# A third tile picked by matmuls in one step of four of a graph attention layer

## The chip, the core and the metric

The kernel runs on one core of a Trainium2 chip, in one launch. The metric is the device time of that launch in microseconds (us); the lower the better. The core has five engines that work side by side, each through its own queue of instructions in order: PE (matmuls, with its weight loads shown as a row of their own, PEld), DVE (vector operations), ACT (activations and copies), POOL (here it issues the indirect gathers) and SP (here it issues the other DMAs). They wait for each other by semaphores only. SBUF is the working memory, PSUM the memory that matmuls write to.

## What is computed

A graph has 6250 nodes with 64 features each and 206250 edges (200000 drawn ones and a loop at each node), sorted by destination. For each edge the key and the value of its source, the query of its destination and a projection of its own features make four scores (heads); the messages are summed by destination, added to the node's features and normalised. Cut to what matters:

```python
Qh = (x @ Wq.T + bq).reshape(n, H, D)          # n = 6250, H = 4, D = 16
Kh = (x @ Wk.T + bk).reshape(n, H, D)
Vh = (x @ Wv.T + bv).reshape(n, H, D)
Ee = (edge_attr @ We.T + be).reshape(-1, H, D)
score = (Kh[src] * Qh[dst] * (1.0 / np.sqrt(D)) * Ee).sum(-1)
score = jnp.exp(jnp.clip(score, -5.0, 5.0))
msg = Vh[src] * score[..., None]
wV = jax.ops.segment_sum(msg, dst, num_segments=n)
x = _layernorm(x + wV.reshape(n, H * D), axis=-1)
```

## The kernel before

**Tiles, groups, steps.** The edges are cut into 1612 tiles of 128, one edge to a partition. Eight tiles are a group, two groups (16 tiles) a step; the last eight steps have one group each, so there are 105 steps. The kernel computes k and v of all nodes first and writes them to a table in memory (`kv_tab`).

**Sources by gather.** k and v of a tile's 128 sources come by one indirect DMA for each tile (`gather_kv`, L389 to L393), which POOL issues. They land in one of five step buffers (`kvs`, KVB = 5). In step s the gathers of step s + 4 are put into POOL's queue; the buffer that they go to was read last by the message of step s - 1.

**Sources by matmul.** In the steps s = 4 to 94 (`picks_in`) the last two tiles of step s + 2 get k and v in another way: their rows of x are *picked* by matmuls, and `gather` leaves these tiles out. x is held in SBUF as three bf16 parts that add up to fp32 (`parts`): row 50 p + b of x stands on partition p in block b, with 50 blocks. For a picked tile:

- `sources` (ACT, L449) computes the source number less 50 p for each edge and each p, and `sources_turned` (PE, L458) transposes that into PSUM (`from_b`), so that p is the partition;
- `hots` (DVE, L465) compares it with the 50 block numbers and so makes 50 one-hot matrices of 128 x 128, in two halves of 25, an instruction each;
- `picks` (PE, L475) multiplies each of them with a block of the parts, 50 matmuls that accumulate in `rows3`, also in two halves;
- `picked` (DVE) adds the three parts, `picked_turned` (PE, ACT) transposes the rows, and `picked_kv` (PE, ACT) multiplies them with the weights of k and v and copies the result to the step's buffer.

**The rest of a step.** `spread` (PE, L518) with `onehot_rows` (ACT) makes the one-hot matrices by which `queries` (PE, L558) fetches the queries; `edges` (PE, L377 and L380) computes the projected edge features; `products` and `scores` (DVE, L565 to L574) and an exponential (ACT, L575) make the scores; `message` (DVE, L582) the messages, which `minus` (PE L593, ACT L595) splits into three bf16 parts; `sums` (PE, L601) adds them by destination with the one-hots of `onehot_edges` (DVE, L548), and `add` (DVE, L615) puts them into accumulators. About every second step a block of 128 destinations is complete and is closed (`close`, `spreads`, from L631 on).

**The order.** It is written out by hand in the loop from L671 on, with no scheduler behind it: each engine runs its instructions in the order of the calls. The PSUM tile `edges` writes to has one buffer, so the next step's edges wait for this step's products. The order within a step, with the engine's own work named once each: spread and sums (PE), sources turned (PE), products (DVE), picked (DVE), edges (PE), first picks (PE), scores, add, message (DVE), the second half of the edges and the minus matmuls around the second picks (PE), two hots, the one-hots of the edges and the two hots of the next step (DVE), k and v of the picked rows, third picks, queries, fourth picks (PE), closing (DVE).

Of the kernel before, what the change touches and what calls it, by code (L numbers as in the profile page):

```python
# [7 lines left out]
F32 = mybir.dt.float32  # L8
BF16 = mybir.dt.bfloat16
I32 = mybir.dt.int32  # L10
AF = mybir.ActivationFunctionType
# [3 lines left out]
P = 128  # L15
N = 6250
C = 64
# [21 lines left out]
KVB = 5  # L39
XG = 4  # L40
TB = 8
M0 = 4
PAD = N
SPARE = N + 1
# [13 lines left out]
def groups_of(s):  # L58
    return range(STEPS[s][0], STEPS[s][0] + STEPS[s][1])
# [6 lines left out]

def picks_in(s):
    return M0 <= s <= LAST


def about_where(g):
# [20 lines left out]
def tile_gnn(ctx: ExitStack, tc: tile.TileContext, x, xT, wT, bias, beT, weT, eT, src, dst, dst_rows,  # L92
# [308 lines left out]
    with tc.If(rv == 0) as branch:  # L401

        with tc.tile_pool(name="work", bufs=2) as work, \
# [2 lines left out]
                tc.tile_pool(name="psum", bufs=1, space=bass.MemoryType.PSUM) as psum:  # L406
            TO, OH, PE, PQ, M3, PA = ({} for _ in range(6))
            small = fixed.tile([P, 4 * P], F32, name="small")
            col, from0, from1 = (small[:, i * C:(i + 1) * C].bitcast(BF16) for i in range(3))
            from_b = from0, from1  # L410
            score_all = small[:, 3 * C:3 * C + 2 * G * H]
            pa = small[:, 4 * C:7 * C].rearrange("p (i c) -> p i c", i=3)
            nc.tensor.transpose(col, row_b[:, 0:1].to_broadcast([P, P]), ident_b)

            parts = accp.tile([P, NB, 3, C], BF16, name="parts")
# [6 lines left out]
            for i in range(2):  # L422
                nc.vector.tensor_copy(src_f[:, :, i],
                                      src_i[:, t0 + i:t0 + i + 2 * G * (n_picks - 1) + 1:2 * G])
            pick = fixed.tile([P, 4 * P], F32, name="pick")
            rows3 = pick[:, :6 * C].rearrange("p (k i c) -> p k i c", k=2, i=3)
            HOT, FAR, X = {}, {}, {}
# [15 lines left out]
            def table_parts_rest(b, rest):  # L443
# [2 lines left out]
                nc.scalar.activation(parts[:NX, b:b + n, 1], rest, AF.Copy)  # L446
                nc.vector.tensor_sub(parts[:NX, b:b + n, 2], rest, parts[:NX, b:b + n, 1])

            def sources(s, i):  # L449

                if picks_in(s):
                    FAR[s, i] = work.tile([P, P], BF16, name="far")
                    nc.scalar.activation(FAR[s, i], row50, AF.Identity,
                                         bias=src_f[:, s - M0, i:i + 1], scale=-1.0)

            def sources_turned(s, i):  # L458
                if picks_in(s):
                    nc.tensor.transpose(from_b[i], FAR.pop((s, i)), ident_b)  # L460

            def blocks(h):
# [1 line left out]

            def hots(s, i, h):  # L465

                if picks_in(s):
                    HOT[s, i, h] = work.tile([P, NB // 2, P], BF16, name="hot", bufs=4)
                    shape = [P, NB // 2, P // 2, 2]
                    nc.vector.tensor_tensor(  # L470
                        HOT[s, i, h].rearrange("p b (a c) -> p b a c", c=2),
                        pairs(from_b[i])[:, None].to_broadcast(shape),
                        block2[:, blocks(h), None, :].to_broadcast(shape), op=OP.is_equal)

            def picks(s, i, h):  # L475
                if picks_in(s):
                    hot = HOT.pop((s, i, h))
                    for k in range(NB // 2):
                        b = h * NB // 2 + k
                        nc.tensor.matmul(rows3[:, i], hot[:, k, :], parts[:, b], start=b == 0,  # L480
                                         stop=b == NB - 1)

            def picked(s):

                if picks_in(s):
                    xp = work.tile([P, 2, C], F32, name="xp")
                    nc.vector.tensor_reduce(xp, rows3.rearrange("p k i c -> p k c i"), axis=AX.X,
                                            op=OP.add)
                    X[s] = xp

            def picked_turned(s):
                if picks_in(s):
                    room = psum.tile([P, G, P], F32, name="pb")
                    nc.tensor.transpose(room[:, 0, :], X[s].rearrange("p k c -> p (k c)"), ident)
                    xe = work.tile([P, P], F32, name="xe")
                    nc.scalar.activation(xe, room[:, 0, :], AF.Copy)
                    X[s] = xe, room[:, 4:6, :]

            def picked_kv(s):
                if picks_in(s):  # L500
                    xe, kv = X.pop(s)
                    nc.tensor.matmul(kv, ones_b, bkv_p[:, :2], start=True, stop=False,
                                     skip_group_check=True)
                    nc.tensor.matmul(kv, xe, wkv, start=False, stop=True, skip_group_check=True)  # L504
                    nc.scalar.activation(kvs[(s + 2) % KVB][:, 2 * G - 2:, :], kv, AF.Copy)

            def gather(s):
                for g in groups_of(s):
                    for j in range(tiles_of(g)):
                        if not picks_in(s - 2) or g == STEPS[s][0] or j < G - 2:  # L510
                            gather_kv(g, j)


# [74 lines left out]
            def minus(s, msg, i):  # L588

                n = tiles_in(s)  # L590
                for lo in range(0, n, G):
                    hi = min(n, lo + G)
                    nc.tensor.matmul(msg[:, lo:hi, :], minus_b, M3[s][:, lo:hi, i, :], start=False,  # L593
                                     stop=True, skip_group_check=True)
                nc.scalar.activation(M3[s][:, :n, i + 1, :], msg[:, :n, :], AF.Copy)  # L595
# [75 lines left out]
            for s in range(NS):  # L671
                more = s + 1 < NS
                for g in groups_of(s):
                    if g % LG == 0 and g + 2 * LG < NG:
                        fetch_edges(g // LG + 2)
                if s + 2 < NS:
                    for g in groups_of(s + 2):
                        fetch_queries(g)
                nexts = list(groups_of(s + 1)) if more else []
                if more:  # L680
                    onehot_rows(nexts[0], spread(nexts[0]))
                    onehot_rows_rest(nexts[0])
                if s:
                    sums(s - 1)
                sources_turned(s, 1)
                sources_turned(s + 1, 0)
                if nexts[1:]:
                    onehot_rows(nexts[1], spread(nexts[1]))
                making = [b for b in range(s * 2 * TB, (s + 1) * 2 * TB, TB) if b < NB]
                if making:  # L690
                    rest = table_parts(making[0])
                prod = products(s)
                picked(s - 1)
                if more:
                    edges(s + 1, 0)
                picks(s, 0, 0)
                score = scores(s, prod)
                if nexts[1:]:
                    onehot_rows_rest(nexts[1])
                if s:  # L700
                    add(s - 1)
                msg = message(s, score)
                if s + KVB - 1 < NS:
                    gather(s + KVB - 1)
                picked_turned(s - 1)
                if nexts[1:]:
                    edges(s + 1, 1)
                minus(s, msg, 0)
                hots(s, 1, 0)
                picks(s, 0, 1)  # L710
                minus(s, msg, 1)
                picked_kv(s - 1)
                if not more:

                    close(B - 2)
                    spreads(B - 2)
                hots(s, 1, 1)
                picks(s, 1, 0)
                sources(s + 1, 1)
                sources(s + 2, 0)  # L720
                if more:
                    if nexts[0] * G % KEYS == 0:
                        keys(nexts[0] * G)
                    onehot_edges(s + 1)
                    queries(s + 1)
                picks(s, 1, 1)
                hots(s + 1, 0, 0)
                hots(s + 1, 0, 1)
                if more:

                    while closed < B - 2 and due[closed] <= s:
                        close(closed)
                        spreads(closed)
                        closed += 1
                    if closed in BATCHES and closed > scaled:
                        roots(scaled, closed)
                        scales(scaled, closed)
                        scaled = closed
                    for _ in range(3):
                        if normed < scaled:  # L740
                            norm(normed)
                            normed += 1
                for i, b in enumerate(making):
                    if i:
                        rest = table_parts(b)
                    table_parts_rest(b, rest)
# [175 lines left out]
```

## Time and profile before

| | us |
|---|---|
| median of 3 runs | 1808.31 |
| lowest and highest of them | 1808.10, 1808.62 |
| the profiled execution's own time | 1808.39 |
| its span, from first to last instruction | 1806.6 |

| engine | busy us | share of the span | instructions |
|---|---|---|---|
| PE, matmuls | 1641.5 | 91% | 15751 |
| PE, weight loads | 1370.4 | 76% | 15751 |
| DVE | 1481.7 | 82% | 1695 |
| ACT | 912.0 | 50% | 1313 |
| POOL | 1351.8 | 75% | 1442 |

A group of the page is written as line, engine, operation, output and input by the program's names, count, busy time and mean duration, and then the idle time just before these instructions with what ended it. "issue" there is time in which the engine waited for nothing that the profile shows. Matmuls are pipelined: the duration of one record is longer than the distance to the next, so costs of PE are better read from start to start. A line of the timeline has start, duration and instruction, and in brackets the idle time before it.

### The profile page before, as it was taken

Reading aid. Unit: us, or ns where it says so; the run is one execution under the profiler, and the core shown is the slowest. Engines: PE = TensorE matmul, PEld = TensorE weight load, DVE = VectorE, ACT = ScalarE, POOL = GpSimd, SP = SyncE. Lnnn points to the kernel's source line nnn. Section 1 sums busy time; section 2 is a strip of 40 time slices with the busy share of each in tenths; the row PEclk is TensorE's granted clock in tenths of the full one; section 3 lists DMA queues with packets and bytes.
Section 4 is the critical chain, followed back from the end, with each engine's and each line's share of the span. In section 5 each row is a group of like instructions: output and inputs, shape, how many; then the busy total and the mean of one; then the engine's idle time right before and its main releaser. Section 6 shows DMA issues by size and latency. Waiting matters only on the chain.

```text
span 1806.6 us, 38129 instructions
## 1 busy us (share of the span) xinstructions
PE 1641.5 (91%) x15751; PEld 1370.4 (76%) x15751; DVE 1481.7 (82%) x1695; ACT 912.0 (50%) x1313; POOL 1351.8 (75%) x1442
## 2 busy tenths in 40 slices
PE   8979999999999998999899898989999999999864
PEld 8547888888877777777777787877777778777632
DVE  6459999999988898888888888888988888888554
ACT  4465555555545454544545444455444545445443
POOL 7777777777777777777777777777777777777774
PEclk9968999999999999999999999999999999999855
DMA  8343323333323333332333323323332332332331
GB/s 239 112 120 92 92 80 104 80 101 83 92 79 93 91 84 90 99 81 81 92 91 90 80 79 93 91 79 98 84 92 80 92 91 79 91 91 79 89 79 45
DMA packets 106532, 166.30 MB, mean 92 GB/s; under 512 B 67501, under 2 KB 67822, under 8 KB 106236
## 3 DMA queue, kind: packets, MB, share of 16 engines
q0 software_dynamic: 45760, 92.76, 19.6%
q1 hardware_dynamic: 60204, 70.01, 13.5%
q8 instruction: 125, 2.05, 0.5%
q10 hardware_dynamic: 384, 1.00, 0.3%
q14 instruction: 59, 0.48, 0.1%
HBM read 156.32 MB, written 7.33 MB: 91 GB/s over the span
## 4 chain that ended last, share of the span: by engine, by line
PE 31%; POOL 28%; DVE 19%; issue 14%; DMA 4%; ACT 3%; DVEq 0%; SPq 0%; POOLq 0%; ACTq 0%
POOL kv L391 28%; PE pick L480 15%; DVE hot L470 7%; PE pe L380 4%; DMA kv<-kv_tab,src_i 4%; PE pq L593 2%; DVE prod L565 2%; DVE prod L566 2%; PE small L601 2%; DVE pq L582 2%; DVE small L572 2%; PE pb L518 2%; DVE acc L615 1%; PE pb L504 1%; PE pe L377 1%
## 5 line engine op out<-in xcount | busy, mean ns | idle before, releaser
L391 POOL DMA_INDIRECT kv<-kv_tab,src_i x1398 | 1319.7, 944 | 426.1 <-issue 403.5
L480 PE MATMUL pick<-parts,hot 128*128 128x192 bf16 x9100 | 825.6, 249 | 0.0
L480 PEld LDWEIGHTS <-hot 128*128 128x128 bf16 x9100 | 769.6, 99 | 38.0
L470 DVE TENSOR_TENSOR hot<-small,block 128x3200 bf16<-128x3200 bf16 x364 | 645.9, 1816 | 0.8 <-PE pick L480 0.8
L535 ACT ACTIVATE to<-pb,minus_row 126x1024 bf16<-126x1024 f32 x202 | 222.8, 1103 | 372.7 <-PE pb L518 368.7
L380 PEld LDWEIGHTS pe<-we_sb,et 128*128 128x128 f32 x1612 | 213.2, 206 | 152.9 <-issue 136.8
L595 ACT ACTIVATE msg<-pq 128x1024 bf16<-128x1024 f32 (+2 forms) x210 | 207.8, 990 | 219.7 <-PE pq L593 219.7
L565 DVE TENSOR_TENSOR prod<-kv,pq 128x1024 f32<-128x1024 f32 (+2 forms) x105 | 123.6, 1177 | 191.7 <-DMA kv<-kv_tab,src_i 92.7
L380 PE MATMUL pe<-we_sb,et 128*128 128x128 f32 x1612 | 254.3, 305 | 0.0
L540 ACT ACTIVATE to<-to,one_p 126x1024 bf16<-126x1024 bf16 x202 | 230.6, 1142 | 3.5
L377 PE MATMUL pe<-be_p,ones_b 3*128 3x512 bf16 x202 | 80.0, 396 | 104.8 <-DVE prod L566 104.8
L601 PEld LDWEIGHTS <-of 128*128 128x128 bf16 x1612 | 145.1, 102 | 30.9 <-issue 7.8
L601 PE MATMUL small<-msg,of 128*128 128x192 bf16 x1612 | 161.5, 256 | 0.5 <-ACT msg L595 0.5
L593 PE MATMUL pq<-msg,minus_b 128*128 128x512 bf16 x404 | 128.1, 396 | 30.8 <-ACT msg L585 16.6
L585 ACT ACTIVATE msg<-pq 128x1024 bf16<-128x1024 f32 (+2 forms) x105 | 103.9, 990 | 96.9 <-DVE pq L582 96.9
L572 DVE TENSOR_REDUCE small<-prod 128x64 f32<-128x1024 f32 (+2 forms) x105 | 123.6, 1177 | 13.3 <-PE small L460 7.5
L518 PE MATMUL pb<-key_rows,ident_b 112*128 112x512 bf16 x403 | 127.7, 399 | 2.8 <-ACT to L535 2.8
L566 DVE TENSOR_TENSOR prod<-prod,pe 128x1024 f32<-128x1024 f32 (+2 forms) x105 | 123.6, 1177 | 3.6
L582 DVE TENSOR_TENSOR pq<-kv,small 128x1024 f32<-128x1024 f32 (+2 forms) x105 | 123.5, 1176 | 1.4 <-ACT small L575 1.4
L548 DVE TENSOR_TENSOR of<-small,key 128x2048 bf16<-128x2048 bf16 (+2 forms) x105 | 123.2, 1173 | 0.3
L575 ACT ACTIVATE small<-small 128x64 f32<-128x64 f32 (+2 forms) x105 | 21.7, 207 | 131.0 <-DVE small L574 130.5
L558 PEld LDWEIGHTS <-to 126*128 126x128 bf16 x1612 | 63.5, 101 | 25.1 <-issue 24.9
(128 smaller groups left out, 992.1 us busy)
## 6 DMA issues: line engine op xcount, KB each, us to landing
et<-in_eT SPq DMA_DIRECT2D x100, 512.0 KB
kv<-kv_tab,src_i POOLq DMA_INDIRECT x1398
qw<-q_tab SPq DMA_DIRECT2D x202, 15.8 KB
kv_tab<-kv_sb SPq DMA_DIRECT2D x5, 640.0 KB
q_tab<-q SPq DMA_DIRECT2D x5, 480.0 KB
acc<-in_x SPq DMA_DIRECT2D x48, 32.0 KB
out<-y SPq DMA_DIRECT2D x48, 32.0 KB
raw<-in_x SPq DMA_DIRECT2D x6, 250.0 KB
```

The lines of the kernel that those rows point to most:

```text
L380: nc.tensor.matmul(pe[:, 2 * u:2 * u + 2, :], et[:, u, :], we_sb, start=False, stop=u == n // 2 - 1, skip_group_check=True)
L391: nc.gpsimd.indirect_dma_start(out=kv_of(g)[:, j, :], out_offset=None, in_=kv_tab[:, :], in_offset=bass.IndirectOffsetOnAxis(ap=src_i[:, t ...
L470: nc.vector.tensor_tensor(HOT[s, i, h].rearrange("p b (a c) -> p b a c", c=2), pairs(from_b[i])[:, None].to_broadcast(shape), block2[:, bl ...
L480: nc.tensor.matmul(rows3[:, i], hot[:, k, :], parts[:, b], start=b == 0, stop=b == NB - 1)
L518: nc.tensor.matmul(pb[:, b:b + 4, :], ident_b[:NR2, g // 2:g // 2 + 1].to_broadcast([NR2, P]), key_rows[:, g % 2, b * P:(b + 4) * P], star ...
L535: nc.scalar.activation(TO[g][:, :n, :], pb[:3 * W, :n, :], AF.Square, bias=minus_row3[:3 * W])
L540: nc.scalar.activation(TO[g][:, :n, :], TO[g][:, :n, :], AF.Relu, bias=one_p[:3 * W], scale=-1.0)
L565: nc.vector.tensor_mul(prod[:, :n, :], kvs[s % KVB][:, :n, :C], PQ[s][:, :n, :])
L566: nc.vector.tensor_mul(prod[:, :n, :], prod[:, :n, :], PE[s][:, :n, :])
L593: nc.tensor.matmul(msg[:, lo:hi, :], minus_b, M3[s][:, lo:hi, i, :], start=False, stop=True, skip_group_check=True)
L595: nc.scalar.activation(M3[s][:, :n, i + 1, :], msg[:, :n, :], AF.Copy)
L601: nc.tensor.matmul(PA[s], OH[s][:, j, :], M3[s][:, j], start=j == 0, stop=j == n - 1)
```

## The change

In every fourth step of those that pick (steps 4, 8, ... 92, `picks_third`), a third tile is picked by matmuls, the one ahead of the pair in the buffer, and its gather is left out.

The third tile has an index of its own, 2, in `sources`, `sources_turned`, `hots` and `picks`. Its source numbers have a place of their own in the PSUM tile `small` (so `score_all` and `pa` move up by one place), and a table `src_f3`. Its picks run after the first tile's and before the second's and write to the second tile's region of `rows3`. Therefore the second tile's picks, which otherwise stand around the queries, come at the end of such a step, behind a new reduction `picked_third` on DVE, which reads the region before it is used again. The third tile's first hot stands at the end of the step before, behind the next step's two; its second hot stands between the two of the second tile. The reduced rows share one tile with those of the pair; they are transposed by a matmul of their own, and k and v of all three come from one bias matmul and two products and leave PSUM by one copy. The buffers for `hot` go from 4 to 6 and those for `far` from 2 to 3.

```diff
+def picks_third(s):
+    return picks_in(s) and s % THIRD == 0
+
+def is_picked(g, j):
+    s = g // 2
+    return picks_in(s - 2) and g == groups_of(s)[-1] and j >= (G - 3 if picks_third(s - 2) else G - 2)
...
-            col, from0, from1 = (small[:, i * C:(i + 1) * C].bitcast(BF16) for i in range(3))
-            from_b = from0, from1
-            score_all = small[:, 3 * C:3 * C + 2 * G * H]
-            pa = small[:, 4 * C:7 * C].rearrange("p (i c) -> p i c", i=3)
+            col, *from_b = (small[:, i * C:(i + 1) * C].bitcast(BF16) for i in range(4))
+            score_all = small[:, 4 * C:4 * C + 2 * G * H]
+            pa = small[:, 5 * C:8 * C].rearrange("p (i c) -> p i c", i=3)
...
+            def wanted(s, i):
+                return picks_third(s) if i == 2 else picks_in(s)
...
-                    FAR[s, i] = work.tile([P, P], BF16, name="far")
+                    FAR[s, i] = work.tile([P, P], BF16, name="far", bufs=3)
...
-                    HOT[s, i, h] = work.tile([P, NB // 2, P], BF16, name="hot", bufs=4)
+                    HOT[s, i, h] = work.tile([P, NB // 2, P], BF16, name="hot", bufs=6)
...
-                        nc.tensor.matmul(rows3[:, i], hot[:, k, :], parts[:, b], start=b == 0,
-                                         stop=b == NB - 1)
+                        nc.tensor.matmul(rows3[:, min(i, 1)], hot[:, k, :], parts[:, b],
+                                         start=b == 0, stop=b == NB - 1)
+
+            def picked_third(s):
+                if picks_third(s):
+                    X[s] = work.tile([P, 3, C], F32, name="xp")
+                    nc.vector.tensor_reduce(X[s][:, 0], rows3[:, 1].rearrange("p i c -> p c i"),
+                                            axis=AX.X, op=OP.add)
...
+                    if picks_third(s):
+                        nc.tensor.transpose(room[:C, 1, :], X[s][:, 0], ident)
+                    nc.scalar.activation(xe[:, 0], room[:, 0, :], AF.Copy)
+                    if picks_third(s):
+                        nc.scalar.activation(xe[:C, 1], room[:C, 1, :], AF.Copy)
...
+                    lo = 0 if picks_third(s) else 1
+                    nc.tensor.matmul(kv[:, lo:], ones_b, bkv_p[:, lo:3], start=True, stop=False,
+                                     skip_group_check=True)
+                    nc.tensor.matmul(kv[:, 1:], xe[:, 0], wkv, start=False, stop=lo == 1,
+                                     skip_group_check=True)
+                    if lo == 0:
+                        nc.tensor.matmul(kv[:, 0], xe[:C, 1], wkv[:C, 0], start=False, stop=True,
+                                         skip_group_check=True)
+                    nc.scalar.activation(kvs[(s + 2) % KVB][:, 2 * G - 3 + lo:, :], kv[:, lo:], AF.Copy)
...
-                        if not picks_in(s - 2) or g == STEPS[s][0] or j < G - 2:
+                        if not is_picked(g, j):
                             gather_kv(g, j)
...
                 sources_turned(s + 1, 0)
+                sources_turned(s + 1, 2)
...
                 hots(s, 1, 0)
+                hots(s, 2, 1)
                 picks(s, 0, 1)
+                picks(s, 2, 0)
                 minus(s, msg, 1)
+                picks(s, 2, 1)
                 picked_kv(s - 1)
...
                 hots(s, 1, 1)
-                picks(s, 1, 0)
+                if not picks_third(s):
+                    picks(s, 1, 0)
                 sources(s + 1, 1)
                 sources(s + 2, 0)
+                sources(s + 2, 2)
...
-                picks(s, 1, 1)
+                if not picks_third(s):
+                    picks(s, 1, 1)
                 hots(s + 1, 0, 0)
+                picked_third(s)
+                if picks_third(s):
+                    picks(s, 1, 0)
+                    picks(s, 1, 1)
                 hots(s + 1, 0, 1)
+                hots(s + 1, 2, 0)
```

More of the change, by code (lines that the diff above doesn't have):

```diff
@@ L41 @@
 TB = 8
+THIRD = 4
 M0 = 4
@@ L424, in tile_gnn @@
                                       src_i[:, t0 + i:t0 + i + 2 * G * (n_picks - 1) + 1:2 * G])
+            src_f3 = accp.tile([P, (LAST - M0) // THIRD + 1], F32, name="src_f3")
+            assert M0 % THIRD == 0
+            nc.vector.tensor_copy(src_f3, src_i[:, t0 - 1:t0 + 2 * G * (LAST - M0):2 * G * THIRD])
             pick = fixed.tile([P, 4 * P], F32, name="pick")
@@ L447, in table_parts_rest @@
                 nc.vector.tensor_sub(parts[:NX, b:b + n, 2], rest, parts[:NX, b:b + n, 1])
+            def wanted(s, i):
+                return picks_third(s) if i == 2 else picks_in(s)
             def sources(s, i):
-                if picks_in(s):
-                    FAR[s, i] = work.tile([P, P], BF16, name="far")
-                    nc.scalar.activation(FAR[s, i], row50, AF.Identity,
-                                         bias=src_f[:, s - M0, i:i + 1], scale=-1.0)
+                if wanted(s, i):
+                    FAR[s, i] = work.tile([P, P], BF16, name="far", bufs=3)
+                    at = src_f3[:, (s - M0) // THIRD:][:, :1] if i == 2 else src_f[:, s - M0, i:i + 1]
+                    nc.scalar.activation(FAR[s, i], row50, AF.Identity, bias=at, scale=-1.0)
             def sources_turned(s, i):
-                if picks_in(s):
+                if wanted(s, i):
                     nc.tensor.transpose(from_b[i], FAR.pop((s, i)), ident_b)
@@ L465, in hots @@
             def hots(s, i, h):
-                if picks_in(s):
-                    HOT[s, i, h] = work.tile([P, NB // 2, P], BF16, name="hot", bufs=4)
+                if wanted(s, i):
+                    HOT[s, i, h] = work.tile([P, NB // 2, P], BF16, name="hot", bufs=6)
                     shape = [P, NB // 2, P // 2, 2]
@@ L475, in picks @@
             def picks(s, i, h):
-                if picks_in(s):
+                if wanted(s, i):
                     hot = HOT.pop((s, i, h))
@@ L479, in picks @@
                         b = h * NB // 2 + k
-                        nc.tensor.matmul(rows3[:, i], hot[:, k, :], parts[:, b], start=b == 0,
-                                         stop=b == NB - 1)
+                        nc.tensor.matmul(rows3[:, min(i, 1)], hot[:, k, :], parts[:, b],
[5 more added lines that the diff above has]
+                                            axis=AX.X, op=OP.add)
             def picked(s):
                 if picks_in(s):
[L486 to L489, printed above, removed]
+                    if s not in X:
+                        X[s] = work.tile([P, 3, C], F32, name="xp")
+                    nc.vector.tensor_reduce(X[s][:, 1:], rows3.rearrange("p k i c -> p k c i"),
+                                            axis=AX.X, op=OP.add)
             def picked_turned(s):
@@ L493, in picked_turned @@
                     room = psum.tile([P, G, P], F32, name="pb")
[L494 to L497, printed above, removed]
+                    xe = work.tile([P, 2, P], F32, name="xe")
+                    nc.tensor.transpose(room[:, 0, :], X[s][:, 1:].rearrange("p k c -> p (k c)"), ident)
+                    if picks_third(s):
[3 more added lines that the diff above has]
+                        nc.scalar.activation(xe[:C, 1], room[:C, 1, :], AF.Copy)
+                    X[s] = xe, room[:, 4:7, :]
             def picked_kv(s):
@@ L501, in picked_kv @@
                     xe, kv = X.pop(s)
-                    nc.tensor.matmul(kv, ones_b, bkv_p[:, :2], start=True, stop=False,
+                    lo = 0 if picks_third(s) else 1
+                    nc.tensor.matmul(kv[:, lo:], ones_b, bkv_p[:, lo:3], start=True, stop=False,
                                      skip_group_check=True)
-                    nc.tensor.matmul(kv, xe, wkv, start=False, stop=True, skip_group_check=True)
-                    nc.scalar.activation(kvs[(s + 2) % KVB][:, 2 * G - 2:, :], kv, AF.Copy)
+                    nc.tensor.matmul(kv[:, 1:], xe[:, 0], wkv, start=False, stop=lo == 1,
[4 more added lines that the diff above has]
+                    nc.scalar.activation(kvs[(s + 2) % KVB][:, 2 * G - 3 + lo:, :], kv[:, lo:], AF.Copy)
             def gather(s):
```

## The prediction

> **What bounds the kernel now.** I read the page's groups first, then the starts of the first product of each step (DVE, L565) along the timeline, then busy time by stretch, then single steps. The groups of the page:
>
> ```profile
> L391 POOL DMA_INDIRECT kv<-kv_tab,src_i x1398 | 1319.7, 944 | 426.1 <-issue 403.5
> L480 PE MATMUL pick<-parts,hot 128*128 128x192 bf16 x9100 | 825.6, 249 | 0.0
> L470 DVE TENSOR_TENSOR hot<-small,block 128x3200 bf16<-128x3200 bf16 x364 | 645.9, 1816 | 0.8 <-PE pick L480 0.8
> ```
>
> POOL waits for no consumer: its idle time is 0.3 us of issue after each gather. Its first gather starts at 43.1 and its last at 1787.7, so the pitch is 1744.6 / 1397 = 1.249 us. That chain, and 18.0 us behind it, is the span. A step with two picked tiles has 14 gathers: 17.48 us.
>
> But the kernel did not always run at that pace. The first product starts at 145.47 in step 4, 176.34 in step 6, 333.31 in step 16, 474.53 in step 25 and 1680.72 in step 94. From step 6 to 25 that is 15.69 us a step; from 25 to 94 it is 17.48. Early on the steps work off the gathers fetched ahead; from step 25 they wait for new ones. Two stretches, one of each kind:
>
> ```profile
> core 0: us, PE busy (x) PEld busy (x) DVE busy (x) ACT busy (x) POOL busy (x), PEclk, DMA share, GB/s
> ...
> 165.00:300.00 135.00, 135.00 (x1416) 115.60 (x1414) 127.59 (x130) 73.73 (x104) 102.07 (x109) 1.00 0.33 88
> ...
> 900.00:1050.00 150.00, 138.34 (x1422) 117.66 (x1422) 126.84 (x128) 73.16 (x103) 113.42 (x121) 0.99 0.31 84
> ```
>
> In the first, PE has no idle time and DVE 5.5%. So there are two limits: POOL's 17.48 us, and a computing pace of 15.69 us a step that shows only early. The second decides the change. The timeline of steps 8 and 9 shows what sets it:
>
> ```profile
> 207.73 1.22 DVE L565 TENSOR_TENSOR prod<-kv,pq 128x1024 f32<-128x1024 f32 x1 [0.29 <-DMA kv<-kv_tab,src_i]
> ...
> 210.35 0.39 PE L377 MATMUL pe<-be_p,ones_b 3*128 3x512 bf16 x1
> ...
> 222.20 1.21 DVE L565 TENSOR_TENSOR prod<-kv,pq 128x1024 f32<-128x1024 f32 x1
> 223.45 1.22 DVE L566 TENSOR_TENSOR prod<-prod,pe 128x1024 f32<-128x1024 f32 x1
> ...
> 223.71 0.60 PE L518 MATMUL pb<-key_rows,ident_b 112*128 112x512 bf16 x2
> ...
> 226.10 0.39 PE L377 MATMUL pe<-be_p,ones_b 3*128 3x512 bf16 x1
> ...
> 237.28 2.23 PE L480 MATMUL pick<-parts,hot 128*128 128x192 bf16 x25
> 237.63 0.59 DVE L631 TENSOR_REDUCE y<-acc 128x64 f32<-128x256 f32 x1
> ...
> 239.13 1.22 DVE L565 TENSOR_TENSOR prod<-kv,pq 128x1024 f32<-128x1024 f32 x1 [0.29 <-DMA kv<-kv_tab,src_i]
> 239.35 0.60 PE L518 MATMUL pb<-key_rows,ident_b 112*128 112x512 bf16 x2
> ```
>
> PE goes round in 239.35 - 223.71 = 15.64 us without a wait. DVE takes 14.47 us in step 8, and 16.93 in step 9, which ends with a closing of a block (L631 on). So PE, after prod's start, reaches the edges (L377, which need prod's second half read) 2.62 us later behind a closing, and 3.90 us later otherwise.
>
> **The change, part by part.** Steps 4, 8, ... 92 are thirds: 23.
>
> *Removed:* 23 gathers of 1.249 us: 28.7 us of POOL. If POOL stays the bound, the span is 1777.9.
>
> *Added on PE, each third:* 50 picks. 25 of them take 2.06 us from start to start of what follows (237.28 to 239.35): 4.13. One more transpose of sources 0.06 (two take 0.11), one of the picked rows 0.21 (229.47 to 229.68), one fp32 product of 128 columns 0.25 (two matmul records a call, and L380's eight take 0.99), 128 more columns of bias 0.05. Sum **4.70 us**. PE has no idle time at the computing pace, so nothing hides it.
>
> *Added on DVE:* two hots of 1.73 us (start to start), one of them at the end of the step before the third; the new reduction, near L659's 0.35 us. Sum 3.8 us. The second hot of the third lies beside PE's 4.1 us of picks. The first stands between a step's last hot and the next prod, so prod, and with it the edges, come 1.73 us later, while PE arrives only 0.06 later. Behind a closing the cover was 2.62 - 2.48 = 0.14 us (prod's second half ends 2.48 after prod's start): PE waits 1.5 us there, and 0.1 at the minus matmuls (L593), which stand behind message and ACT's copy. In the other parity the cover is 3.90 - 2.48 - 0.06 = 1.36: PE waits 0.3, and again 0.1. Behind the waiting L377 in PE's queue stand all picks of that step.
>
> *The new order:* picks of the second tile wait until the third's rows are read. PE has picked_kv and queries (0.74 + 0.47 us) to do meanwhile; the reduction comes 0.1 us after the last third pick if DVE is there, and DVE is, by about 0.5 us, with three hots and the one-hot of edges done. Cost: between 0 and 0.4 us; I take 0. ACT gets 0.2 + 0.13 + 0.33 us per third, and is idle 50%: nothing. The hot buffers go from 4 to 6, far from 2 to 3: no new wait. SP's and POOL's queues are moved past nothing; 23 fewer gathers cannot slow the rest. Start-up gets one copy on DVE, 0.2 us.
>
> So a third costs 4.70 + 1.65 = **6.35** us behind a closing, 4.70 + 0.45 = **5.15** otherwise. A step has 62 rows and a block 128, so closings drift: from the code's due times they end the odd steps up to 19 and from 55 to 85, the even ones otherwise. 13 thirds stand behind one, 10 do not: 13 x 6.35 + 10 x 5.15 = 134 us. The 32 normalisations at steps 34 to 39 and 67 to 72 (0.33 us each on DVE), hidden now by waits for gathers, cost about 4 of their 10 us. PE's own idle can lower its clock, as here:
>
> ```profile
> 932.09 0.37 PE L377 MATMUL pe<-be_p,ones_b 3*128 3x512 bf16 x1 [2.28 <-DVE prod L566]
> ...
> 932.39 1.93 PE L380 MATMUL pe<-we_sb,et 128*128 128x128 f32 x8
> ...
> 934.11 3.15 PE L480 MATMUL pick<-parts,hot 128*128 128x192 bf16 x25
> ```
>
> After 2.28 us of idle time the eight edge matmuls took 1.93 us, where they mostly take 1.16, and the picks 3.15 for 2.23. The Trainium skill (TensorE: Matmul & The Clock Gate, "HAM oscillation — how this bites in real kernels") asks for no idle gap over some 3.4 us; by it stalls of 1.5 us cost no clock. By the rows they sometimes do: of 21 waits of L377 between 1.4 and 2.2 us, 3 were followed by slow matmuls, each losing 1.65 us. I go by the rows: 13 x 3/21 x 1.65 = 3 us; every one of the 13 would be 21.
>
> *Sum.* Step 94's prod: 145.5 + 90 x 15.69 + 134 + 4 + 3 = 1698.6, where it now stands at 1680.7. That is 17.26 us a step; POOL's 55 gathers in four steps are 68.7 us, 17.17 a step. So PE, no longer POOL, sets the pace. POOL is not held up: at step 4 it is three steps ahead of prod and may be four.
>
> The tail gets shorter, because its gathers are there already. Today step 95's prod waits 6.5 us for them and step 96's 8.6, and steps 94 to 97 take 47.1 us (1680.72 to 1727.77). Without: 15.0 (PE's picks of step 94 before the queries of 95), some 11.8 (a step without picks; today its queries start 12.0 us behind its prod, 1711.29 - 1699.28), 12.3 as today (it waits for queries): 39.1, so 8.0 saved. Of the eight single steps two wait for gathers, 1.4 us longer each than the others': 2.8. Span: 1806.6 + (1698.6 - 1680.7) - 8.0 - 2.8 = 1813.7. The profiled execution's own time is 1808.39, 1.8 over its span; the median of the runs is 1808.31, so the two stand for each other. **1815 us**, 0.4% slower.
>
> A rule against this reading of PE: the Trainium skill (Perfetto Trace Analysis, "Identifying the Most-Contended Engine") judges PE by its weight loads, not its matmul row. They are busy 115.60 of 135 us, so 14%, or 8.8 us in four steps, would be free, over the 4.7 added. Then PE hides the third tile, and POOL's 1779.7 follows. The starts speak against it: PE's groups follow each other without a wait for 15.64 us, and picks stream 192 columns over weights of 128, so their loads cannot fill the row.
>
> **Rivals.** *POOL stays the bound:* 1777.9 + 1.8 = 1779.7. For it: 1.8 us of slack a step now (7.1 in four) against 4.7. Against: those early 37 us of lead were spent at 15.7, and the end would need a third at about 4.2.
>
> *PE takes the work but not the stalls,* DVE making up its late hot: a third is 4.70, step 94 at 145.5 + 1412 + 108 + 4 = 1669.6, the tail from there 115.1: 1784.7 + 1.8 = 1786.5. It needs DVE to be over 1.5 us ahead behind a closing; the rows show 0.14.
>
> *The clock falls with each late edge:* 18 us more, 1833. It decides if more than half of the 13 do so; the 2.1 to 2.7 us idles before slow matmuls speak for it, the 18 of 21 against.
>
> *That it gathers as much as before* is excluded: the same condition decides gather and pick.
>
> **How the numbers follow.** Chances: mine 0.5, POOL's bound 0.10, no stalls 0.22, clock 0.18. An error of 0.4 us in a third is 9 us, so my own range is 1805 to 1825. The range to 1785 and 1833 leaves out POOL's bound and the far half of the clock's case. A measurement of this kernel tells 0.2%, 3.6 us: faster means under 1804.7. Faster: 0.32 from two rivals and 0.06 of mine. Same: 0.17 of mine. Slower: the rest, 0.45.
>
> **What would show it.** 1375 gathers; prod no longer waiting for gathers between steps 25 and 94; PE's row full throughout; PE's edges waiting 1.5 us for prod's second half in steps 56 to 84 that are thirds; four steps in 69.3 or 68.0 us by parity of closings; POOL's last gather near 1759. If prod still waits for gathers at step 50, the third is cheaper than I make it; if picks of the second tile wait for the new reduction, dearer.

## The result and the profile after

| | before | changed |
|---|---|---|
| median us | 1808.46 (1808.10 to 1808.62, 4 runs) | 1824.35 (1822.82 to 1830.11, 4 runs) |
| ratio | | 1.0094, interval 1.0082 to 1.0106 |
| span of the profiled execution | 1806.6 | 1824.0 |

The change makes the kernel 0.9% slower. The forecast was 1815, 0.4% slower, and its span of 1813.7 is 10.3 us short. Ten of the twelve runs below fell on chips on which the kernel before took 3009 to 3125 us, and two, "e1b" and "e4b", on one on which it took 1811.75; so times are compared only within one chip, through the kernel before. Single steps of e4b can still be laid beside those of the changed kernel: where nothing slows PE, four steps take the same in both traces to 0.02 us (steps 44 to 48: 68.03, steps 56 to 60: 69.22).

The page's groups of the changed kernel (lines have moved: the gathers are L402, picks L496, hots L486):

```profile
L402 POOL DMA_INDIRECT kv<-kv_tab,src_i x1375 | 1297.9, 944 | 438.0 <-issue 395.3
L496 PE MATMUL pick<-parts,hot 128*128 128x192 bf16 x10250 | 913.6, 247 | 0.0
L486 DVE TENSOR_TENSOR hot<-small,block 128x3200 bf16<-128x3200 bf16 x410 | 727.0, 1814 | 0.0
```

The counts are those of the change: 23 gathers less, 1150 picks and 46 hots more. The stretch that was quoted of the kernel before, in busy time by engine:

```profile
900.00:1050.00 150.00, 147.27 (x1548) 126.64 (x1548) 137.86 (x141) 76.64 (x110) 113.44 (x121) 1.00 0.32 85
```

PE was busy for 138.34 of these 150 us before. Now it is for 147.27, and DVE for 137.86 instead of 126.84. POOL gathers at the same pitch (121 gathers in these 150 us, as before), but it is no longer waited for. The product of step 50, before and now:

```profile
911.38 1.22 DVE L565 TENSOR_TENSOR prod<-kv,pq 128x1024 f32<-128x1024 f32 x1 [2.81 <-DMA kv<-kv_tab,src_i]
...
940.05 1.22 DVE L597 TENSOR_TENSOR prod<-kv,pq 128x1024 f32<-128x1024 f32 x1 [0.52 <-issue]
```

At the end of the run POOL waits itself, for DVE's message to free a buffer. Its waits, by what ended them (us in total, times, longest):

```profile
POOL kv L402 <- issue: 395.3, 1297, 0.3
POOL kv L402 <- DVE pq L614: 21.1, 7, 6.6
```

Where the time goes is seen in steps 56 and 60, both thirds behind a closing. Their products and the second half of them on DVE (L597, L598), PE's first edges (L388, L391) and the picks after them:

```profile
1043.40 1.22 DVE L597 TENSOR_TENSOR prod<-kv,pq 128x1024 f32<-128x1024 f32 x1 [0.29 <-DMA kv<-kv_tab,src_i]
...
1044.66 1.22 DVE L598 TENSOR_TENSOR prod<-prod,pe 128x1024 f32<-128x1024 f32 x1
...
1045.93 0.37 PE L388 MATMUL pe<-be_p,ones_b 3*128 3x512 bf16 x1 [1.52 <-DVE prod L598]
1046.23 1.16 PE L391 MATMUL pe<-we_sb,et 128*128 128x128 f32 x8
...
1047.23 2.23 PE L496 MATMUL pick<-parts,hot 128*128 128x192 bf16 x25
...
1115.14 0.37 PE L388 MATMUL pe<-be_p,ones_b 3*128 3x512 bf16 x1 [1.52 <-DVE prod L598]
1115.44 1.16 PE L391 MATMUL pe<-we_sb,et 128*128 128x128 f32 x8
...
1116.44 3.88 PE L496 MATMUL pick<-parts,hot 128*128 128x192 bf16 x25
```

Both wait 1.52 us for the product that the new hot has pushed back. After the same wait the 25 picks take 2.23 us in one step and 3.88 in the other. The next prod comes 16.86 us after the first of these two (1043.40 to 1060.26) and 18.31 us after the second (1112.62 to 1130.93). Why the same wait has two outcomes is shown by the granted clock, in the last section.

### The profile page after: what moved, and what is told of

It reads as the page before. It is cut to its first block, busy times and chain, and to the rows that moved or that the text cites. A ratio compares the mean times of both kernels' runs of the same rounds, so it can differ in the third digit from the quotient of the medians.

```text
span 1824.0 us, 40750 instructions
## 1 busy us (share of the span) xinstructions
PE 1730.8 (95%) x16993; PEld 1461.2 (80%) x16993; DVE 1571.2 (86%) x1765; ACT 925.0 (51%) x1359; POOL 1330.0 (73%) x1419
## 5 line engine op out<-in xcount | busy, mean ns | idle before, releaser
L402 POOL DMA_INDIRECT kv<-kv_tab,src_i x1375 | 1297.9, 944 | 438.0 <-issue 395.3
L496 PE MATMUL pick<-parts,hot 128*128 128x192 bf16 x10250 | 913.6, 247 | 0.0
L496 PEld LDWEIGHTS <-hot 128*128 128x128 bf16 x10250 | 856.5, 98 | 38.5
L486 DVE TENSOR_TENSOR hot<-small,block 128x3200 bf16<-128x3200 bf16 x410 | 727.0, 1814 | 0.0
L391 PEld LDWEIGHTS pe<-we_sb,et 128*128 128x128 f32 x1612 | 208.3, 202 | 80.8 <-issue 70.2
L391 PE MATMUL pe<-we_sb,et 128*128 128x128 f32 x1612 | 248.8, 300 | 0.0
L597 DVE TENSOR_TENSOR prod<-kv,pq 128x1024 f32<-128x1024 f32 (+2 forms) x105 | 123.2, 1173 | 50.1 <-PE pq L590 27.5
L598 DVE TENSOR_TENSOR prod<-prod,pe 128x1024 f32<-128x1024 f32 (+2 forms) x105 | 123.6, 1178 | 3.6
L388 PE MATMUL pe<-be_p,ones_b 3*128 3x512 bf16 x202 | 80.2, 397 | 32.0 <-DVE prod L598 32.0
L647 DVE SCALAR_TENSOR_TENSOR acc<-small,above,acc 128x192 f32<-128x192 f32 x103 | 43.0, 417 | 43.5 <-ACT small L607 42.8
```

The costliest lines, as they stand in the source:

```text
L391: nc.tensor.matmul(pe[:, 2 * u:2 * u + 2, :], et[:, u, :], we_sb, start=False, stop=u == n // 2 - 1, skip_group_check=True)
L402: nc.gpsimd.indirect_dma_start(out=kv_of(g)[:, j, :], out_offset=None, in_=kv_tab[:, :], in_offset=bass.IndirectOffsetOnAxis(ap=src_i[:, t ...
L486: nc.vector.tensor_tensor(HOT[s, i, h].rearrange("p b (a c) -> p b a c", c=2), pairs(from_b[i])[:, None].to_broadcast(shape), block2[:, bl ...
L496: nc.tensor.matmul(rows3[:, min(i, 1)], hot[:, k, :], parts[:, b], start=b == 0, stop=b == NB - 1)
L598: nc.vector.tensor_mul(prod[:, :n, :], prod[:, :n, :], PE[s][:, :n, :])
```

## The experiments

**The third's first hot in its own step (e1, e1b).** It no longer stands ahead of a prod.

```diff
-                hots(s, 1, 0)
-                hots(s, 2, 1)
+                hots(s, 2, 0)
+                hots(s, 1, 0)
+                hots(s, 2, 1)
...
-                hots(s + 1, 2, 0)
```

> The third tile's first hot stands in its own step, ahead of the second tile's first hot, and no longer at the end of the step before; everything else is the changed kernel. Theory (the hot ahead of prod holds PE up at the edges, and the stall costs clock): PE's wait at L388 of 1.52 and 0.29 us in the thirds goes, a quad of steps takes 62.8 + 4.7 = 67.5 us in both parities, step 94's prod comes at about 1671 (1706 in the changed kernel), time about 1790. Rival (it is PE's added work, with the waits only a place where it shows): a third costs what it does now, time 1818 to 1826. Second rival (DVE is then late for the next step instead, as the third's own step has one hot more): PE waits at L388 in the step after a third, time 1805 to 1825.

> The same kernel as in the first run with the third's first hot in its own step, on a chip where the kernel before should take 1808 us again (in the earlier run it took 3009, with PE short of instructions, which tells nothing about waits between engines). Theory (the hot ahead of prod holds PE up at the edges): no waits of 1.52 and 0.29 us in the thirds, 67.5 us for four steps in both parities, step 94's prod at about 1671, time about 1790. Rival (PE's added work alone makes the time): 1818 to 1826. Second rival (DVE is late in the step after the third instead): 1805 to 1825, with PE's waits at L388 one step later.

Measured in e1b: 1801.19 us where the kernel before takes 1811.75, ratio 0.9943 (0.9926 to 0.9959). That is faster than both kernels, and it does the same work as the changed one, which stands at 1.0094 against before. Of the waits at the edges in the thirds one of 0.98 us is left, in step 68, where DVE also normalises; in the steps behind a third there is none, so DVE did not come late there, as the second rival had it (1805 to 1825). But the time is not the 1790 expected. Step 56, end of the third (L503 is the new reduction):

```profile
1045.66 0.63 PE L590 MATMUL pq<-qw,to 126*128 126x64 bf16 x16
...
1046.36 0.35 DVE L503 TENSOR_REDUCE xp<-pick 128x64 f32<-128x192 f32 x1
...
1046.76 3.46 PE L496 MATMUL pick<-parts,hot 128*128 128x192 bf16 x40 [0.47 <-DVE xp L503]
```

With one hot more ahead of it on DVE, the reduction comes after the queries are issued, and PE's late picks wait for it:

```profile
PE pick L496 <- DVE xp L503: 10.7, 23, 1.2
```

These 23 waits add up to 10.7 us, the size of the difference between 1801 and 1790; step 94's prod, expected at 1671, comes at 1680.93. Four steps take 68.12 us behind closings (1030.16 to 1098.28), where the wait is mostly 0.47, and 67.89 otherwise (483.65 to 551.54), where it is 0.25. Without the wait, and less the 62.79 that four steps take in the early stretch of the kernel before (207.73 to 270.52), that leaves 4.86 and 4.85 us for PE's own work, close to the 4.70 put down. So the added work of PE costs what its matmuls cost; the 1.52 us were the place of the hot, as the first theory has it. The rival that PE's work alone makes the time (1818 to 1826) falls.

Where the gain arises is worth a look: step 94's prod comes at 1680.93 in e1b and at 1680.72 in the kernel before. Up to there the third tile only breaks even, give or take the 3.3 us by which the two chips differ for the kernel before; it is the tail behind, without its waits for gathers, that is shorter (117.9 us against 125.9).

**PE kept busy in that wait (e4, e4b).** In the 13 thirds behind a closing the sums are computed twice.

```diff
                     sums(s - 1)
+                    if s in (*range(4, 21, 4), *range(56, 85, 4)):
+                        sums(s - 1)
```

> The changed kernel, where in the 13 thirds behind a closing the sums of the step before are computed twice on PE (16 matmuls, 1.32 us, the same result), in the time in which PE waits 1.52 us for prod. The wait at the edges ends when it ended before; only PE is not idle. Theory (idle time there lowers the clock in 5 or 6 of the 13, 1.65 us each): no slow picks behind these waits, 7 to 10 us less, 1814 to 1817, and the runs scatter less than 1822.8 to 1830.1. Rival (the clock falls for another reason, or the slow picks cost nothing): no change, 1822 to 1826, or slower by up to 13 x 1.32 = 17 us if the added matmuls are not hidden.

> The same kernel as in the first run with the sums computed twice in the 13 thirds behind a closing, again on a chip where the kernel before should take 1808 us. Theory (idle time of 1.52 us lowers PE's clock in 5 or 6 of the 13 thirds, 1.65 us each): no slow picks behind these waits, 7 to 10 us less than the changed kernel, 1814 to 1817, and little scatter. Rival (the clock falls for another reason): no change, 1822 to 1826; up to 17 us slower if the added matmuls are not hidden.

Measured in e4b: 1816.68 us (1813.51 to 1820.09, 13 runs), ratio 1.0028 (1.0019 to 1.0036); the changed kernel has 1.0094. 13 x 16 more matmuls make it 0.66 points, some 12 us, faster; 7 to 10 were expected. Step 60 again:

```profile
1110.05 1.22 DVE L597 TENSOR_TENSOR prod<-kv,pq 128x1024 f32<-128x1024 f32 x1 [0.29 <-issue]
...
1112.58 0.37 PE L388 MATMUL pe<-be_p,ones_b 3*128 3x512 bf16 x1 [0.20 <-DVE prod L598]
1112.88 1.16 PE L391 MATMUL pe<-we_sb,et 128*128 128x128 f32 x8
1113.88 2.23 PE L496 MATMUL pick<-parts,hot 128*128 128x192 bf16 x25
```

The edges start 2.53 us after prod, as in the changed kernel's step 56 (1045.93 - 1043.40 = 2.53). The stall as such is still there; only its idle time is filled. Of the picks behind the edges none is slow in the whole trace, and the granted clock is full from 148 to 1720 us. In the changed kernel six groups are slow, in the thirds at steps 8, 16, 60, 68, 72 and 80. Each of the six four-step stretches that start there is 1.44 to 1.46 us longer than in e4b, 8.7 us in all, and the others are the same to about 0.1 us but for the first, from step 4, which is 0.36 us longer in e4b; step 94's prod comes at 1697.83 instead of 1706.21, 8.4 us earlier. That the idle time lowers the clock, and that this makes the difference, is shown. The expected small scatter did not come: 6.6 us over 13 runs, about as much as the changed kernel's 7.3 over four. What else scatters is open.

**The gathers alone (e2, e2b)** and **the gathers put back (e3, e3b, e3c).** The first is the kernel before without the third tiles' gathers; their k and v are old values of the buffer. The second is the changed kernel with them; PE's third k and v are not copied out.

```diff
 # e2
-                        if not picks_in(s - 2) or g == STEPS[s][0] or j < G - 2:
+                        left = G - (3 if s % 4 == 2 else 2)
+                        if not picks_in(s - 2) or g == STEPS[s][0] or j < left:
 # e3
-                        if not is_picked(g, j):
+                        if not picks_in(s - 2) or g == STEPS[s][0] or j < G - 2:
...
-                    nc.scalar.activation(kvs[(s + 2) % KVB][:, 2 * G - 3 + lo:, :], kv[:, lo:], AF.Copy)
+                    nc.scalar.activation(kvs[(s + 2) % KVB][:, 2 * G - 2:, :], kv[:, 1:], AF.Copy)
```

> The kernel before, with the 23 gathers of the third tiles left out and nothing put in their place (their k and v are then old values of the buffer). Theory (POOL's gathers set the pace of the kernel before): 23 x 1.249 = 28.7 us less, time 1779.7. Rival (part of the gain was never to be had, since the computing pace or the tail binds next): a gain of 10 to 20 us only, time 1788 to 1798.

> The changed kernel with the 23 gathers put back; k and v of the third tile are still computed on PE, but not copied to the step's buffer. Theory (PE sets the pace of the changed kernel, POOL's relief is not used): 1820 to 1830, as the changed kernel, in which POOL is even held up 21 us by full buffers. Rival (the gathers taken off still pay for a part of the added work): 10 to 29 us slower than the changed kernel, 1834 to 1853.

> The same kernel as in the first run, the kernel before with the 23 gathers of the third tiles left out and nothing in their place, on a chip where the kernel before should take 1808 us. Theory (POOL's gathers set the pace of the kernel before): 28.7 us less than the kernel before, 1780 to 1783. Rival (another limit binds at once): 10 to 20 us less only.

> The same kernel as in the earlier runs with the 23 gathers put back, on a chip where the kernel before should take 1808 to 1812 us. Theory (PE sets the pace of the changed kernel, the gathers taken off bring nothing): as the changed kernel, 1820 to 1830. Rival (they still pay for a part of the added work): 10 to 29 us more, 1834 to 1853.

All five fell on chips where the kernel before takes 3009 to 3125 us: e2 0.9910 (0.9894 to 0.9927) and e2b 0.9776 (0.9757 to 0.9795), e3 1.0300, e3b 1.0258 and e3c 1.0301 of it. There PE waits for its own instructions and POOL for free buffers, so POOL does not set the pace, and these ratios say nothing of the question. What 23 gathers are worth alone at the usual pace is left open; that they are no longer needed in the changed kernel is read from its trace (POOL held up 21.1 us by full buffers, from step 25 to 94 DVE never stands idle before a product for more than 0.7 us, where 1 to 3 us were common before).

**The reduction ahead of the next hot as well (e6, e6c), and that in one step of five (e7).**

```diff
 # e6, on top of e1
-                hots(s + 1, 0, 0)
                 picked_third(s)
+                hots(s + 1, 0, 0)
 # e7, on top of e6
-THIRD = 4
+THIRD = 5
...
-    return picks_in(s) and s % THIRD == 0
+    return picks_in(s) and (s - M0) % THIRD == 0
```

> The kernel with the third's first hot in its own step, and the new reduction now ahead of the next step's first hot on DVE instead of behind it. Theory (what is left over PE's own 4.7 us a third is the wait of PE's late picks for that reduction, 0.47 us in each of the 23 thirds): the wait goes, 67.5 us for four steps, 10 us less than with the hot alone moved, time 1788 to 1793 where the kernel before takes 1808 to 1812. Rival (the reduction is then waited for by DVE, which comes late to prod in turn): no gain, 1798 to 1804. Floor by POOL's gathers: 1780 to 1784.

> As the kernel with both moves, but with the third tile in one step of five (19 thirds in place of 23). Theory (the time is the larger of POOL's chain and of the computing pace): PE's four thirds less are 19 us, POOL's four gathers more 5 us; the computing pace gives some 1771, POOL's chain 1785 to 1789, so POOL is the bound again, prod waits for gathers, and the time is 1785 to 1789, about that of one step in four. Rival (the computing pace still decides): 1771 to 1780.

> The same kernel as in the earlier run of both moves, on a chip where the kernel before should take 1808 to 1812 us. Theory (what the first move left is PE's wait of 0.47 us for the new reduction in each third): no such wait, 67.5 us for four steps, some 10 us less than with the hot alone moved (1801), 1788 to 1793. Rival (DVE waits for the reduction instead and comes late to prod): 1798 to 1804.

These too fell on such chips: e6 1.0037 (1.0025 to 1.0048), e6c 1.0175 (1.0155 to 1.0195), e7 1.0048 (1.0029 to 1.0066) of the kernel before, beside 1.0194 for e1 and 1.0256 for e4 on the chip with 3009 us. e1 shows what such ratios are worth: one and the same kernel is 1.9% slower than before there and 0.6% faster in e1b. Whether the second move brings the last 10 us is not decided. Fastest of what was measured at the usual pace is e1b.

## Why the prediction came out as it did

**The bound.** Right: with the third tiles PE sets the pace, and the early stretch of the kernel before, at 15.69 us a step, was the one to build on. The rivals with a chance of 0.10 (POOL as the bound) and 0.22 (a third without stalls) lost; the latter needed DVE ahead by 1.5 us, and it is not. The measured 1824.35 lies at the very edge of the range 1805 to 1825, and halfway from 1815 to the 1833 of the rival by which the clock falls with each late edge. So the bound and the stalls were read rightly, but that the time fell inside the range is in part luck.

One side argument of the prediction does not hold: that loads of 128 columns cannot fill PE's row while picks stream 192. In the kernel before, the picks' loads were busy for 769.6 us of the 825.6 of their matmuls. What pulls the loads' share down to 86% are chiefly the matmuls of 512 columns (L518, L593, L377: 92.3 us of loads for 334.6 of matmuls). That the free time of the load row could not be used is shown all the same, by the 4.9 us that a third costs on PE without any stall.

**The cost of a third.** Right in size. The waits at the edges were put at 1.5 us behind a closing and 0.3 otherwise; they are 1.51 to 1.52 in nine of 13, and 0.28 to 0.36 in seven of ten. Four steps were to take 69.3 or 68.0 us; they take 69.22 (steps 56 to 60, 1043.40 to 1112.62) and 68.03 (steps 44 to 48, 837.42 to 905.45), where the clock holds. The agreement is a little better than its parts: the prediction's own sum gives 69.1 and 67.9, PE's own work is about 4.9 us and not 4.70 (69.22 - 62.79 - 1.52 = 4.91), and the waits of 0.1 us at the minus matmuls did not come. The new reduction made DVE wait (0.31 us in step 56) and PE not, as said.

**The clock.** This is the step that failed, as a size: "13 x 3/21 x 1.65 = 3 us". The price of one event was near (the picks of step 60 lose 1.65 us, 3.88 for 2.23, and the four steps 1.44), and the rows were the better guide than the Trainium skill's rule (TensorE: Matmul & The Clock Gate, "HAM oscillation — how this bites in real kernels") of no gap over some 3.4 us, which would have made it nothing; six waits of 1.52 to 1.87 us were enough here. The rate was wrong: 3 of 21 waits in the kernel before, 6 of 13 here. (The trace has 25 such waits from step 25 to 94, with 3 slow groups behind them, so the rate was 0.12 to 0.14.) e4b, which differs from the changed kernel by nothing but the matmuls in this idle time, brings step 94's prod 8.4 us forward, 5.4 more than the term had. The term's 3 us taken off, the forecast for step 94 without any clock event was 1695.6, or 1697.1 with the start of step 4 where it was found (146.99 for 145.5); e4b has 1697.83.

**The tail.** From step 94's prod to step 97's 39.1 us were forecast; it is 41.6 (1706.21 to 1747.84). Step 94 takes 15.6 us for the 15.0 put down, and the two steps without picks about 13 each for 11.8 and 12.3. The single steps behind came as said: 76.2 us from there to the end, forecast 76.0 (78.8 before, less 2.8).

The sum of the misses: 1.5 at the start, 5.4 for the clock, 0.7 more up to step 94, 2.5 in the tail, 0.2 behind it: 10.3 us. "POOL is not held up" was right up to about 1695 us and wrong after it, when its gathers of the last steps wait for free buffers; so the sign given, a last gather near 1759, did not come (it starts at 1777.8).

So the change trades POOL's 28.7 us for PE's work, which with the stalls was put at 134 us. Steps 4 to 94 took 1535.3 us before (145.47 to 1680.72), and at PE's pace would have taken 90 x 15.69 = 1412: 123 us to spare. The changed kernel takes 1559.2 there (146.99 to 1706.21), 147 more than 1412, and so loses. With the hot in its own step, and almost no idle time at the edges, it is 125 (143.77 to 1680.93): even, and the shorter tail makes the gain of 0.6%.

## What to carry to other kernels

A stretch in which the bound engine does not bind, such as a start with data fetched ahead, shows the pace of the next one; a change that takes work off the bound is to be priced against that pace, at once with the stalls that the new instructions cause in each parity of the loop. An instruction added between the last work of one step and the one that another engine waits for costs that engine its full length less the lead that was there: the hot of 1.73 us cost 1.52 where the lead was small and 0.29 where it was larger. The same instruction moved ahead of its own, later consumer took these waits away, but pushed the next waited-for instruction back, by up to half a microsecond in most steps. Idle time of PE can cost more than itself: filling 1.3 us of it in 13 steps with useless matmuls was worth 0.66%.

## What the runs showed of the hardware

**The clock after a short wait.** Of the 13 waits, the three of 1.78 to 1.87 us are followed by slow matmuls, and so are three of the nine of 1.51 to 1.52; the one of 1.31 is not. So the length alone does not decide. The granted clock does show what goes with it. In the changed kernel's trace between 165 us and step 94 it is full but for six stretches of 3.41 us at half, and the distances between their starts (218.96, 358.90, 1116.66, 1256.61, 1328.29, 1468.24) are whole multiples of 3.41 us. They lie on one grid; the traces of the kernel before, e1b and e4b have such a grid too, at another offset. Cut along this grid, steps 56 and 60 read (stretch and length; PE, PEld, DVE, ACT and POOL busy; the granted clock; DMA share and GB/s):

```profile
1041.57:1044.99 3.42, 2.84 (x29) 2.20 (x27) 2.96 (x7) 2.38 (x3) 2.51 (x4) 1.00 0.43 86
1044.99:1048.40 3.41, 2.47 (x24) 2.16 (x24) 3.10 (x6) 1.51 (x3) 2.64 (x3) 1.00 0.62 197
1048.40:1051.81 3.41, 3.37 (x30) 2.59 (x28) 3.41 (x5) 2.00 (x4) 2.66 (x3) 1.00 0.21 57
...
1113.25:1116.66 3.41, 1.89 (x14) 1.29 (x13) 3.38 (x4) 1.84 (x2) 2.60 (x3) 1.00 0.77 215
1116.66:1120.08 3.42, 3.42 (x25) 3.25 (x23) 3.11 (x6) 2.19 (x3) 2.50 (x4) 0.50 0.15 40
```

In step 56 an edge of the grid cuts the wait: PE is idle 0.58 us on one side and 0.94 on the other, and the clock stays full. In step 60 the wait lies whole in one stretch, and the next is granted at half. All six half-clock stretches follow one in which PE is idle for 1.50 us or more; of the others only two come to that (1.50 and 1.49, in steps 12 and 20, where the wait begins within 0.05 us of an edge). In the kernel before every stretch with more than 1.71 us idle is followed by half clock, and from full clock none with less than 1.69 is; in e1b and e4b the most idle stretches have 1.08 and 1.34 us, and the clock stays full up to step 94. So the idle time within one stretch of the grid goes with the loss, with a border at 1.5 to 1.7 us. No run shifted a wait along the grid on purpose, and that part is read, not tested. As an estimate from these numbers, a wait of 1.52 us falls whole into a stretch of 3.41 in 55% of cases, some 7 of 13; 6 were slow. The rate taken from the kernel before could not show this.

**PE short of instructions.** On the chips where the kernel before takes 3009 us and more, PE stands still with nothing in the profile that it waits for, and its instructions then start some 0.7 us or a multiple of that apart. Busy time of the engines in stretches of e1 there, with the columns as above:

```profile
1490.00:1499.00 9.00, 8.54 (x82) 6.74 (x80) 8.35 (x6) 4.46 (x8) 6.60 (x7) 1.00 0.37 102
1499.00:1506.50 7.50, 2.01 (x12) 0.76 (x11) 0.00 (x0) 0.00 (x0) 5.67 (x7) 0.79 0.20 52
1506.50:1518.60 12.10, 10.36 (x79) 8.51 (x79) 6.60 (x9) 4.85 (x6) 0.03 (x1) 0.71 0.04 9
1518.60:1526.00 7.40, 7.40 (x76) 6.24 (x76) 7.40 (x5) 3.72 (x7) 5.67 (x6) 1.00 0.17 44
1526.00:1538.40 12.40, 2.58 (x17) 1.01 (x14) 1.36 (x5) 0.43 (x2) 7.56 (x8) 0.69 0.35 95
```

POOL gathers from 1490.6 to 1506.5 and from 1518.6 to 1535.8. PE runs on for some 8 us after the first gather, then gets one instruction or a few at a time (12 in 7.5 us, where it had 82 in 9), and recovers 2 to 3 us after the last gather. There its picks read:

```profile
1507.48 0.64 PE L496 MATMUL pick<-parts,hot 128*128 128x192 bf16 x3 [1.77 <-issue]
1508.88 3.04 PE L496 MATMUL pick<-parts,hot 128*128 128x192 bf16 x18 [0.76 <-issue]
```

A supply of instructions that comes behind the gathers' packets would fit, and so would the gain of 28 and 70 us from 23 gathers less in e2 and e2b. Nothing shows it, though: the 135 large packets that the profile counts as instructions take 0.3% of the DMA engines' span in e1 (3073.5 us) and 0.5% in e1b (1798.8 us), the same time in either within rounding. Why some chips show this and others, with gathers in flight all the time, do not is open.
